# A graph layer on one core: fewer row loads on SP, more on ACT, and a block's own rows asked for a block earlier

## The chip, the cores and the metric

One core of a Trainium2 chip. The metric is the device time of one execution in microseconds (us), the median of three runs. The engines have these names: PE (TensorE, matmuls), DVE (VectorE), ACT (ScalarE), POOL (GpSimd) and SP (SyncE, which computes nothing and issues DMAs). ACT and POOL also issue DMAs, each in its own in-order queue, between their other instructions.

## The reference

12,500 nodes with 128 features each, 200,000 edges sorted by their target node. A normalized copy of the nodes is averaged over the edges that reach each node, and a small network follows, whose result is added to x:

```python
h = jnp.maximum(_layernorm(x, axis=-1), 0.0)
msgs = h[src]
agg = jax.ops.segment_sum(msgs, dst, num_segments=n)
deg = jax.ops.segment_sum(ones, dst, num_segments=n)
agg = agg / jnp.maximum(deg, 1.0)[:, None]
g = jax.nn.relu(agg @ Wg + h @ Ws + bg)          # 128 -> 128
g = jnp.tanh(g @ W1 + b1)                        # 128 -> 512
g = jnp.tanh(g @ W2 + b2)                        # 512 -> 512
out = x + g @ W3 + b3                            # 512 -> 128
```

## The kernel before

The kernel first computes h for all nodes and writes it to a table in DRAM, `htab` (L231 to L249). Then it goes over the edges in 1563 chunks of 128 (`for c in range(NCH)`, L662). A chunk needs 128 rows of `htab`, one for each edge, by the edge's source. DVE makes a one-hot matrix of the chunks' targets, eight chunks at a time (`onehot`), and PE multiplies rows by one-hot into a sum per target node (`add`, L438). Since the edges are sorted, 64 chunks reach about one block of 512 nodes; chunks whose targets straddle two blocks go into a sum of their own, `edge`.

The rows of a chunk come in one of four ways:

- for most chunks, by one indirect DMA of POOL (`gather`, L311, L313), into one of `AHEAD` = 44 row buffers; a gather waits until PE has used the buffer's last rows;
- for the ten groups of eight chunks for which `raw(c)` holds (between chunks 256 and 656), by gathers from x itself, made ahead of all else (L149 to L157);
- for the chunks in `slow_s`, by SP: 128 DMAs of one row (512 bytes) each, `srows`, four to a step;
- for the chunks in `slow_a`, by ACT in the same way, `arows`.

L86 to L100 choose the last two: from chunk 120 on, of every `EACH` + 1 chunks one goes to SP, and of every `EACH_A` + 1 chunks one to ACT. The addresses of single rows are loaded into registers, 32 at a time (`row_loads`, L340 to L356; the load of offsets, from `place`, is L347). L681 to L688 pace these loads: after so many gathered chunks that 128 rows fit evenly into the distance between two such chunks, `next(loading)` issues four more. SP's queue thus holds the single rows of `srows` and, between them in program order, the large DMAs: the blocks' h (`own`, `hb`, 256 KB), the blocks' x (`own_part`, `xb`) and the stores of the output (`store`, L639, called at L665; from chunk `QUICK` = 1312 on, a store enters the queue as soon as its sum has been written in the program). ACT's queue holds the `arows` between its activations and copies.

A block's own rows of h are needed with features on the partitions. `own(s)` loads them from `htab` (L499), `own_turned(s)` transposes them on PE (`pt`, L303 in the profile, which is the helper's line) and copies them out on ACT (`hT`, L510). L706 to L709 call these in the middle of each block's chunks: the next block is turned, and the block after it is loaded. So one block's time, 64 chunks, lies between a block's load and its transposes in the program:

```python
        if c % span == span // 2 and (c // span + 1) * BLK < N:
            own_turned(c // span + 1)
            if (c // span + 2) * BLK < N:
                own(c // span + 2)
```

The layers of earlier blocks are interleaved with the chunks: one step of `go_on` (L647) every two chunks up to `QUICK`, and by estimated times after it. Matmuls, ACT's instructions and SP's DMAs keep the order in which the program writes them; the tile framework's scheduler decides how the engines' orders interleave, and gives each DMA of SP and ACT one of eight semaphores in turn, on which it waits for the DMA that had it last.

A second path, `general`, is taken only where an edge falls outside its window; it isn't in these runs.

Of the kernel before, what the change touches and what calls it, by code (L numbers as in the profile page):

```python
# [22 lines left out]
F32 = mybir.dt.float32  # L23
# [8 lines left out]
P = 128  # L32
EPS = 1e-5
CPR = 16
BLK = 512
# [2 lines left out]
NRAW = 10  # L38
RAW0 = 256
STEP = 40  # L40
AHEAD = 44
SLOW0 = 120
EACH = 58
EACH_A = 76
TOGETHER = 4
LOADS = 32
LATE = 12
# [13 lines left out]
def windowed(ctx, tc, x, src, dst, Wg, Ws, bg, W1, b1, W2, b2, W3, b3, out, flag):  # L61
    nc = tc.nc
    N, D = x.shape
# [18 lines left out]
    def raw(c):  # L82
        return RAW0 <= c < RAW1 and (c - RAW0) % STEP < GRP


    slow_s, slow_a = [], []  # L86
    ns, na = 0, EACH // 2
    for c in range(SLOW0, NCH - 12):
        if raw(c):
            continue  # L90
        if ns <= 0:
            slow_s.append(c)
            ns = EACH
        elif na <= 0 and c < QUICK + EACH_A:
            slow_a.append(c)
            na = EACH_A
        else:
# [25 lines left out]
    rows_one = ctx.enter_context(tc.tile_pool(name="rows_one", bufs=4))  # L123
    rows_in = ctx.enter_context(tc.tile_pool(name="rows_in", bufs=AHEAD))
    ps_c = ctx.enter_context(tc.tile_pool(name="ps_c", bufs=1, space=PSUM))
# [56 lines left out]
    def centre(pool, xt, k, stats, bufs=2):  # L182
        nc.vector.tensor_reduce(stats[:, 0], xt, AX.X, ALU.add)
        nc.vector.scalar_tensor_tensor(xt, spread(stats[:, 0], k), -1.0 / D, xt, op0=ALU.mult, op1=ALU.add)
        sq = pool.tile([P, k, D], F32, name=f"sq{k}", bufs=bufs)
        if bufs > 1:
            nc.scalar.activation(sq, xt, AF.Square)
        else:
            nc.vector.tensor_tensor(sq, xt, xt, op=ALU.mult)
        nc.vector.tensor_reduce(stats[:, 1], sq, AX.X, ALU.add)  # L190

    def factors(stats):
        nc.scalar.activation(stats[:, 1], stats[:, 1], AF.Sqrt, bias=eps, scale=1.0 / D)
        nc.vector.reciprocal(stats[:, 1], stats[:, 1])
# [98 lines left out]
    ml = ctx.enter_context(tc.tile_pool(name="ml", bufs=2))  # L293
# [14 lines left out]
    def sp_dma(*a):  # L308
        tc.keep_in_program_order(nc.sync.dma_start(*a))  # L309
# [48 lines left out]
    def raw_stats(i):  # L358
        return stats_raw[:, :, i * GRP : (i + 1) * GRP]

    def raw_scaled(i):
        h = raw_rows[i]
        scale(h, h, GRP, raw_stats(i))
        for j in range(GRP):
            rows_t[RAW0 + i * STEP + j] = h[:, j]
# [12 lines left out]
    def onehot(g):  # L378
        k = min(GRP, NCH - g * GRP)
        lo, w = window(g * GRP)  # L380
        is_raw = raw(g * GRP)
        oh = ed.tile([P, GRP, W_RAW], F32, name="ohr", bufs=2) if is_raw else oh_bufs[g % OHS]
        if not is_raw and w < oh_w[g % OHS]:
            nc.vector.memset(oh[:, :, w : oh_w[g % OHS]], 0.0)
            oh_w[g % OHS] = w
        nc.vector.tensor_tensor(  # L386
            oh[:, :k, :w], lane[:, None, :w].to_broadcast([P, k, w]),
            dloc[:, g * GRP : g * GRP + k][:, :, None].to_broadcast([P, k, w]), op=ALU.is_equal,
        )
        ohs[g] = oh  # L390
        step, n = (oh.shape[2], w) if is_raw else (PITCH - per, w + per * (k - 1))
        cnt = ed.tile([P, PITCH], BF16, name="cnt", bufs=2)
        part, row, col = oh.ap
        shifted = bass.AP(tensor=oh.tensor, offset=oh.offset, ap=[part, [col[0], n], [step * col[0], k]])
        with nc.allow_low_precision(reason="whole numbers up to the windows that reach a node"):
            nc.vector.tensor_reduce(cnt[:, :n], shifted, AX.X, ALU.add)  # L396
            for b, (n0, m) in enumerate(blocks):
                a0, a1 = max(lo, n0), min(lo + n, n0 + m)
                if a0 < a1:
                    if b not in counts:  # L400
                        counts[b] = ed.tile([P, BLK], BF16, name="deg", bufs=3) if m > P else ed.tile(
                            [P, P], BF16, name="deg_s", bufs=4
                        )
                        nc.vector.memset(counts[b][:, :m], 0.0)
                    d = counts[b][:, a0 - n0 : a1 - n0]
                    nc.vector.tensor_tensor(d, d, cnt[:, a0 - lo : a1 - lo], op=ALU.add)  # L406
# [10 lines left out]
    def count(b):  # L417

        n, m = blocks[b]
        dg = flat(ps_m.tile([P, 4, P], F32, name="pm"))  # L420
        pe.matmul(dg[:, :m], ones, counts.pop(b)[:, :m], start=True, stop=True)
        rd = ml.tile([P, BLK], F32, name="rd", bufs=3)
        nc.vector.tensor_scalar(rd[:, :m], dg[:, :m], 1.0, None, op0=ALU.max)  # L423
        nc.vector.tensor_reduce(total[:, b : b + 1], dg[:1, :m], AX.X, ALU.add)  # L424
        nc.vector.reciprocal(rd[:, :m], rd[:, :m])  # L425
        rds[b] = rd
# [66 lines left out]
    def own(s):  # L493

        n0 = s * BLK
        n = min(BLK, N - n0)
        k = -(-n // P)
        hb = ml.tile([P, BLK // P, D], F32, name="hb", bufs=2)
        sp_dma(hb[:, :k], htab[n0 : n0 + k * P, :].rearrange("(t p) d -> p t d", p=P))  # L499
        owns[s] = hb  # L500

    def own_turned(s):

        k = -(-min(BLK, N - s * BLK) // P)
        hb = owns.pop(s)
        pt = ps_t.tile([P, BLK // P, P], F32, name="pt")
        for t in range(k):
            pe.transpose(pt[:, t, :], hb[:, t, :], ident)
        hT = ml.tile([P, BLK], F32, name="hT", bufs=3)
        act.copy(hT[:, : k * P], pt[:, :k, :].rearrange("p t n -> p (t n)"))  # L510
        hTs[s] = hT
# [124 lines left out]
    span = BLK // per  # L636
    now = at = 0

    def store(upto):  # L639
        while stores and stores[0][0] <= upto:  # L640
            sp_dma(*stores.pop(0)[1:])
# [5 lines left out]
    def go_on(w):  # L647
        nonlocal now
        if w:
# [3 lines left out]
            if w[1] is None:  # L653
                work.remove(w)

    own(0)
    own(1)
    own_turned(0)
    onehot(0)
    onehot(1)  # L660
    counted = 0
    for c in range(NCH):  # L662
        g = c // GRP
        at = c
        store(c if c >= QUICK else c - LATE)  # L665
        if c % GRP == 0 and g + 2 < ngrp:
            onehot(g + 2)
            if raw((g + 2) * GRP):
                raw_scaled(((g + 2) * GRP - RAW0) // STEP)
            if 2 <= g < 2 + NRAW:  # L670
                centre(ed, raw_rows[g - 2], GRP, raw_stats(g - 2), bufs=1)
            if g == 2 + NRAW:
                factors(stats_raw)

        while c % GRP == GRP // 2 and counted < len(blocks) and reach[counted][-1] // GRP <= g + (c >= QUICK):
            count(counted)
            counted += 1
        while nxt < len(order) and nxt < behind + AHEAD:
            gather(order[nxt])
            nxt += 1  # L680
        if not raw(c) and c not in slow:  # L681
            behind += 1
            batch = behind * P // (EACH * TOGETHER)
            if behind > SLOW0 - 3 * EACH and batch > (behind - 1) * P // (EACH * TOGETHER):
                next(loading, 0)
            batch = behind * P // (EACH_A * TOGETHER)
            if behind > 48 and batch > (behind - 1) * P // (EACH_A * TOGETHER):
                next(loading_a, 0)  # L688
        if c >= QUICK:

            there = 7.5 + 1.251 * (NRAW * GRP + order.index(c)) if c not in slow else 0
            while soonest() and max(now, soonest()[2]) < there:
                go_on(soonest())
            now = max(now, there) + 0.27
        add(c)

        lead = LEAD if c < QUICK else 2
        if done < len(blocks) and (c - lead if across[done] else c) >= reach[done][-1]:
            quick = reach[done][-1] + LEAD >= QUICK

            prev, older = (i if i >= 0 and reach[i][-1] + LEAD < QUICK else None for i in (done - 1, done - 2))
            older = None if quick and prev is None else older
            work.append([layers(done, prev, older), 0, 0, 0, quick and blocks[done][1] <= P])
            done += 1

        if c % span == span // 2 and (c // span + 1) * BLK < N:  # L706
            own_turned(c // span + 1)
            if (c // span + 2) * BLK < N:
                own(c // span + 2)  # L709
        if c < QUICK:  # L710
            if c % 2 == 0:
                go_on(work[0] if work else None)
        if c == QUICK:
            for b, (_, n) in enumerate(blocks):
                if n < BLK:
                    own_part(b)
# [379 lines left out]
```

## Time and profile before

| | |
|---|---|
| Runs | 2626.2 us median (2613.55 to 2628.77) |
| Profiled execution | 2637.74 us |
| Its span, first to last instruction | 2635.9 us |
| PE busy | 1242.7 us (47%) |
| PE weight loads (PEld) | 826.4 us (31%) |
| DVE busy | 1148.4 us (44%) |
| ACT busy | 217.6 us (8%) |
| POOL busy | 1446.6 us (55%) |
| srows, issued by SP | 2944 DMAs of 0.5 KB |
| arows, issued by ACT | 1920 DMAs of 0.5 KB |
| rows, gathered by POOL | 1445 indirect DMAs |

How to read what follows. A group line names the source line, the engine, the operation, and the tiles written and read with the count; after the bar stand busy time in us and the mean of one in ns, and after the next bar the engine's idle time just before these instructions with what ended most of it. A line of the waits is "who <- for whom: us in total, times, the longest". A timeline line gives start and duration in us, the engine, and equal instructions merged with their count; in brackets stands the idle time ahead and what ended it. SPq and ACTq are the queues in which SP and ACT issue DMAs; issuing isn't counted as busy. A line of one source line's answer gives the shortest, median and longest duration in ns and the first and last start in us.

### The profile page before, as it was taken

Reading aid. Unit: us, or ns where it says so; the run is one execution under the profiler, and the core shown is the slowest. Engines: PE = TensorE matmul, PEld = TensorE weight load, DVE = VectorE, ACT = ScalarE, POOL = GpSimd, SP = SyncE. Lnnn points to the kernel's source line nnn. Section 1 sums busy time; section 2 is a strip of 40 time slices with the busy share of each in tenths; the row PEclk is TensorE's granted clock in tenths of the full one; section 3 lists DMA queues with packets and bytes.
Section 4 is the critical chain, followed back from the end, with each engine's and each line's share of the span. In section 5 each row is a group of like instructions: output and inputs, shape, how many; then the busy total and the mean of one; then the engine's idle time right before and its main releaser. Section 6 shows DMA issues by size and latency. Waiting matters only on the chain. (4 is left out here: it accounts for less than half of the span.)

```text
span 2635.9 us, 24714 instructions
## 1 busy us (share of the span) xinstructions
PE 1242.7 (47%) x4838; PEld 826.4 (31%) x4838; DVE 1148.4 (44%) x1143; ACT 217.6 (8%) x352; POOL 1446.6 (55%) x1533
## 2 busy tenths in 40 slices
PE   0224334264466446545635535445244545555658
PEld 0113223142234224323323323223122323333437
DVE  5816843443454455434344343343423435334342
ACT  1100000000000001000000000000000000011012
POOL 7666665554464446546646556455554556555660
PEclk9996667686677778767767767667676777777878
DMA  6611111111121111211111111112111111121220
GB/s 173 177 44 45 50 47 41 46 41 39 43 56 44 43 47 49 53 45 50 52 47 46 50 46 49 43 38 52 45 44 45 42 49 49 44 62 46 59 61 14
DMA packets 128694, 139.69 MB, mean 53 GB/s; under 512 B 35036, under 2 KB 103294, under 8 KB 128336
## 3 DMA queue, kind: packets, MB, share of 16 engines
q0 software_dynamic: 48800, 100.04, 15.0%
q1 hardware_dynamic: 72654, 33.65, 4.6%
q10 hardware_dynamic: 7076, 4.32, 0.6%
q14 instruction: 123, 1.01, 0.1%
q8 instruction: 41, 0.67, 0.1%
HBM read 125.07 MB, written 12.82 MB: 52 GB/s over the span
## 5 line engine op out<-in xcount | busy, mean ns | idle before, releaser
L313 POOL DMA_INDIRECT rows<-htab,scol x1445 | 1368.7, 947 | 1104.0 <-PE agg L300 445.9
L300 PE MATMUL pm<-h,w 128*128 128x512 f32 (+4 forms) x1344 | 709.2, 625 | 256.2 <-issue 102.2
L386 DVE TENSOR_TENSOR oh<-shared,dloc 128x1152 f32<-128x1152 f32 (+2 forms) x186 | 244.4, 1320 | 1089.1 <-remote 409.0
L396 DVE TENSOR_REDUCE cnt<-oh 128x200 bf16<-128x1600 f32 (+2 forms) x186 | 522.9, 2817 | 3.7
L300 PEld LDWEIGHTS agg<-oh,rows 128*128 128x128 f32 x2068 | 374.7, 224 | 351.6 <-issue 328.9
L300 PE MATMUL agg<-oh,rows 128*128 128x144 f32 (+3 forms) x2068 | 400.7, 323 | 123.6 <-issue 105.8
L300 PEld LDWEIGHTS pm<-h,w 128*128 128x128 f32 x1344 | 241.5, 219 | 304.0 <-issue 139.1
L303 PE MATMUL pt<-ident,hb 128*128 128x128 f32 x98 | 25.4, 410 | 486.9 <-DMA hb<-htab 449.8
L300 PE MATMUL edge<-oh,rows 128*128 128x144 f32 (+2 forms) x822 | 176.0, 326 | 97.0 <-issue 95.1
L300 PEld LDWEIGHTS edge<-oh,rows 128*128 128x128 f32 x822 | 157.3, 226 | 203.4 <-issue 197.6
L303 PEld LDWEIGHTS pt<-ident,hb 128*128 128x128 f32 x98 | 16.9, 209 | 493.7 <-issue 486.4
L332 ACT ACTIVATE h<-pm,b2c 128x512 f32<-128x512 f32 (+4 forms) x112 | 70.6, 632 | 857.9 <-remote 202.1
L332 ACT ACTIVATE h<-pm,b1c 128x512 f32<-128x512 f32 (+4 forms) x112 | 69.5, 632 | 367.8 <-DMA arows<-htab 96.1
L153 POOL DMA_INDIRECT raw<-in_x_dram,rsrc x80 | 77.0, 962 | 25.5 <-issue 24.1
L425 DVE RECIPROCAL rd<-rd 128x512 f32<-128x512 f32 (+4 forms) x28 | 81.8, 2920 | 0.0
L300 PE MATMUL agg<-oh,srows 128*128 128x144 f32 (+1 forms) x32 | 10.9, 438 | 142.9 <-DMA srows<-htab 108.4
L487 DVE TENSOR_TENSOR mT<-agg,sums 128x136 f32<-128x136 f32 (+6 forms) x57 | 15.0, 267 | 141.6 <-remote 55.3
L335 ACT COPY hT<-pt 128x512 f32<-128x512 f32 (+1 forms) x25 | 14.4, 576 | 582.8 <-PE pt L303 393.6
L406 DVE TENSOR_TENSOR deg<-deg,cnt 128x200 bf16<-128x200 bf16 (+5 forms) x279 | 54.0, 220 | 3.4
L423 DVE TENSOR_SCALAR rd<-pm 128x512 f32<-128x512 f32 (+4 forms) x28 | 17.3, 618 | 84.2 <-remote 64.6
L300 PEld LDWEIGHTS agg<-oh,srows 128*128 128x128 f32 x32 | 7.1, 275 | 147.8 <-issue 76.7
L300 PE MATMUL pm<-mT,wg 128*128 128x512 f32 (+4 forms) x56 | 28.7, 596 | 45.0 <-issue 23.0
(79 smaller groups left out, 513.1 us busy)
## 6 DMA issues: line engine op xcount, KB each, us to landing
srows<-htab SPq DMA_DIRECT2D x2944, 0.5 KB
arows<-htab ACTq DMA_DIRECT2D x1920, 0.5 KB
rows<-htab,scol POOLq DMA_INDIRECT x1445
hb<-htab SPq DMA_DIRECT2D x24, 256.0 KB
xb<-in_x_dram SPq DMA_DIRECT2D x23, 256.0 KB
out_dram<-o SPq DMA_DIRECT2D x23, 256.0 KB
htab<-h SPq DMA_DIRECT2D x6, 896.0 KB
xt<-in_x_dram SPq DMA_DIRECT2D x5, 896.0 KB
```

The source lines that it names most:

```text
L153: nc.gpsimd.indirect_dma_start(out=t[:, j, :], out_offset=None, in_=x, in_offset=bass.IndirectOffsetOnAxis(ap=rsrc[:, g, j : j + 1], axis=0),)
L300: tc.keep_in_program_order(nc.tensor.matmul(*a, **k))
L303: tc.keep_in_program_order(nc.tensor.transpose(*a, **k))
L313: nc.gpsimd.indirect_dma_start(out=r, out_offset=None, in_=htab, in_offset=bass.IndirectOffsetOnAxis(ap=scol[:, c : c + 1], axis=0),)
L332: tc.keep_in_program_order(nc.scalar.activation(*a, **k))
L335: tc.keep_in_program_order(nc.scalar.copy(*a))
L386: nc.vector.tensor_tensor(oh[:, :k, :w], lane[:, None, :w].to_broadcast([P, k, w]), dloc[:, g * GRP : g * GRP + k][:, :, None].to_broadcas ...
L396: nc.vector.tensor_reduce(cnt[:, :n], shifted, AX.X, ALU.add)
L406: nc.vector.tensor_tensor(d, d, cnt[:, a0 - lo : a1 - lo], op=ALU.add)
L423: nc.vector.tensor_scalar(rd[:, :m], dg[:, :m], 1.0, None, op0=ALU.max)
L425: nc.vector.reciprocal(rd[:, :m], rd[:, :m])
L487: nc.vector.tensor_tensor(out, s, t, op=ALU.add)
```

## The change

SP gets 19 chunks in place of 23, ACT 18 in place of 15, POOL 1446 gathers in place of 1445. Four row buffers of POOL's are given up (2 KB a partition), and `hb` gets a third buffer (2 KB a partition). A block's h is loaded one block earlier.

```diff
-AHEAD = 44
+AHEAD = 40
 SLOW0 = 120
-EACH = 58
-EACH_A = 76
+EACH = 72
+EACH_A = 64
...
-        hb = ml.tile([P, BLK // P, D], F32, name="hb", bufs=2)
+        hb = ml.tile([P, BLK // P, D], F32, name="hb", bufs=3)
...
     own(0)
     own(1)
+    own(2)
     own_turned(0)
...
             own_turned(c // span + 1)
-            if (c // span + 2) * BLK < N:
-                own(c // span + 2)
+            if (c // span + 3) * BLK < N:
+                own(c // span + 3)
```

## The prediction, made before the changed kernel ran

> **What bounds the kernel now.** I read the page's groups first, then the waits, then a block's timeline, then SP's own waits. The groups show that no compute engine is full:
>
> ```profile
> L313 POOL DMA_INDIRECT rows<-htab,scol x1445 | 1368.7, 947 | 1104.0 <-PE agg L300 445.9
> L303 PE MATMUL pt<-ident,hb 128*128 128x128 f32 x98 | 25.4, 410 | 486.9 <-DMA hb<-htab 449.8
> ```
>
> POOL, the busiest, idles 1104 us, and 446 of them end when PE frees a row buffer. PE idles 487 us before 98 small transposes, and a load of hb ends 450 of them. The list of waits says the same of the others:
>
> ```profile
> PE pt L303 <- DMA hb<-htab: 449.8, 18, 40.1
> POOL rows L313 <- PE agg L300: 445.9, 129, 24.4
> ACT hT L335 <- PE pt L303: 393.6, 17, 39.5
> ...
> PE agg L300 <- DMA srows<-htab: 125.2, 8, 25.7
> ```
>
> Is hb slow, or asked for late? The timeline around one block's transposes answers:
>
> ```profile
> 1155.80 12.32 SPq L309 DMA_DIRECT2D srows<-htab  x28
> 1168.22 0.41 SPq L309 DMA_DIRECT2D hb<-htab  x1
> ...
> 1171.20 1.09 PE L303 MATMUL pt<-ident,hb 128*128 128x128 f32 x4 [38.61 <-DMA hb<-htab]
> ...
> 1172.33 0.58 ACT L335 COPY hT<-pt 128x512 f32<-128x512 f32 x1 [22.41 <-PE pt L303]
> ...
> 1174.75 0.94 POOL L313 DMA_INDIRECT rows<-htab,scol  x1 [20.67 <-PE agg L300]
> ```
>
> PE transposes 3 us after SP issues the load, having stood idle for 38.6 us: the load is quick, SP is late. It is behind because it issues single rows without pause; what it waits for itself is little:
>
> ```profile
> SPq L309 <- DMA arows<-htab: 89.2, 65, 5.7
> SPq L309 <- DMA srows<-htab: 44.4, 92, 1.4
> ```
>
> SP's 2944 row loads run from 114 to 2559 us, 0.83 us each. So the rate at which SP's queue issues is the bound, and PE, ACT and POOL wait in turn behind it. That rate isn't constant. In the stretch above POOL stood still and SP issued 28 rows in 12.3 us; while POOL gathered every 1.25 us from 1602.4 to 1628.6 (21 gathers) SP got through 16:
>
> ```profile
> 1602.33 25.70 SPq L309 DMA_DIRECT2D srows<-htab  x16
> ```
>
> Counted over the timeline: in 78 stretches of eight gathers 1.25 us apart SP issued 1.34 DMAs a gather; in POOL's pauses over 4 us, 733 in 362 us, or 2.02 a us. A check: of 59.8 chunks 58 are gathered, and SP has 128 rows and 2.8 large DMAs (hb, xb, out) to issue. 58 gathers take 72.5 us, in which SP issues 78; the other 53 need 26.3 us of pauses. That gives 98.8 us, or 1.70 us a gather. The blocks between 1171.2 and 2145.6 us took 108.3 us with some 62 gathers: 1.74. The law holds within 3%.
>
> **The change part by part.** *SP's rows.* srows falls from 2944 to 2432 and its loads of row offsets from 92 to 76. A period is now 72 gathers, with 131.4 DMAs on SP. ACT's rows get denser, 1.94 a gather for 1.66; in the counted stretches SP issued 1.40 a gather where ACT issued 1.2 and 1.25 where ACT issued 1.8, so I lower 1.34 to 1.27. 72 gathers take 90 us, in which SP issues 91; the other 40 need 19.8 us. 109.8 us, or 1.525 a gather: 10.3% less than 1.70. SP's law governs from its first row (114 us) to about chunk 1312 (2257 us, that block's transposes), 2143 us: **-221 us**. Bounds: without ACT's influence 1.49 a gather, 12.3%, -264. The other way: when ACT has no rows left (2227 to 2450 us) SP issues 1.53 a us against 1.27 with 0.97 of ACT's, both at the same share of POOL; that is 0.134 us an SP issue, or 0.175 an ACT row. 430 fewer SP rows up to there at 1/2.02 us give -213, and 384 more ACT rows +67: -146. I keep -221, since the stretches are the nearest rows.
>
> The loads of row offsets lie in these counts, so they are not added again. Their row:
>
> ```profile
> L347 SPq TENSOR_LOAD <-place x92: 343/2113/2469, 111.6 to 2536.4; - x92
> ```
>
> By it the 16 that go are 34 of the 221 us. The Trainium skill (Runtime: NRT & Kernel Launch, Instruction fetch mechanics) puts such a load at about 200 ns a register even in bulk; with 32 registers that would be 6.4 us each and 102 us for the 16. The measured 2.1 us decides.
>
> *ACT's rows*, 1920 to 2304. From 260 to 2227 us ACT's timeline holds 1249 us of row issuing without any wait (1880 rows, 0.66 us each), 145 us of ACTIVATEs and copies, and 573 us of waiting. 384 rows more are 254 us, and they fit into that waiting only if PE comes to it earlier. That they do I price at no cost by themselves; the cover is the 573 us. If it doesn't open, the fourth case below applies.
>
> *The two queues' shared semaphores.* In the built program each DMA of SP or ACT waits for one of eight semaphores dealt out in turn over both queues. SP's DMA follows one of ACT's on its semaphore in 861 of 3046 cases (28%), after the change in 864 of 2534 (34%); ACT's follows SP's in 857 of 1979, then 860 of 2362. An SP row that waits so holds up the srows and the hb behind it. Before, that is the 89.2 us above. Bounds: -89 (the waits go when ACT no longer stands before hT) and +89 (they double with a busier ACT). I take **+45**: ACT is fuller, and that decides.
>
> *hb two blocks ahead.* In the built order hb's load stood where its transposes stand; after, 66 to 150 chunk matmuls lie between, and the srows are complete some 70 chunks ahead of their use instead of 1 to 3. PE's 450 us at hb go. I credit them with nothing: while SP is the bound, PE reaches its srows or ACT's late outputs instead, and waits there. The third buffer is free when it is asked for: the block that held it was turned before.
>
> *AHEAD 44 to 40* lets POOL stop 4 gathers (5 us) sooner in a pause of PE. POOL's 1104 idle us cover it; without that cover it is 5 us for each of 25 blocks, 125 us. One gather more costs 1.25 us, hidden alike.
>
> *The tail.* From chunk 1312 a store enters SP's queue as soon as its sum exists (L665), so an SP that has caught up waits for DVE there; all the rows, hb and xb queued behind it wait too. Before, those waits on o come to 20 us. Bounds +20 and, if SP's law holds there too, -25; I take 0.
>
> Sum: -221 + 45 = -176. The profiled execution took 2637.74 us (span 2635.9), 11.5 over the median of the runs. 2637.7 - 176 = 2462, less 11.5: **2450 us**.
>
> A page speaks against all this: the Trainium skill (DMA: Bandwidth & Descriptors, Issuing engines are not separate DMA queues) says that all issuing engines end on the same 16 DMA engines, so that spreading DMAs saves only issue time, usually small beside the transfer. Here the DMA engines are busy 10 to 20% of most slices and issue time is what SP lacks, so I don't follow it; by it only the total would count.
>
> **The rivals.**
> 1. *The forecast*: SP stays the bound at about 1.53 us a gather. 2450, own range 2370 to 2530. For it: SP's queue never rests in the timeline. Chance 0.50.
> 2. *SP falls out of the way* once it runs ahead, and ACT bounds: 2304 x 0.664 + 190 us of its own work in the loop = 1720 us from its first row (206 us), ending at 1926 instead of 2227. -301: 2325. For it: most of PE's idle time is behind SP. Against: SP's law above. POOL's floor is lower still: 1526 gathers x 1.25 + 113 ahead of the loop + 60 behind = 2080. Chance 0.17.
> 3. *The two queues act as one*, by a shared path or by the semaphores, and only their total counts: 4864 to 4736 row loads, 2.6% of 2445 us, -64: 2562. For it: SP slows when ACT issues more. Against: it slows by a quarter of a DMA for each of ACT's, not by one. Chance 0.18.
> 4. *Slower: ACT becomes the path.* Its 254 us more stand ahead of activations in one in-order queue, and PE waits for these. It decides if ACT's 573 us of waiting shrink by less than 254. If only the 163 us ahead of hT's copy go, the kernel is 91 us slower: 2717. For it: ACT's issues are already stretched to 0.66 us. Against: PE waits for ACT's h only 32 us now. Chance 0.13; and 0.02 that the row and hb edits cancel.
>
> **How the numbers follow.** About 1% is what a measurement of this kernel can tell from no change. 1 and 2 and most of 3 are faster by more: 0.81. Within 1%, between 2600 and 2652: what is left of 3 and the cancelling, 0.06. Slower: 0.13. The range takes in 2 below and 3 above with their scatter, 2300 to 2600, and leaves out 4 and the ends of 2.
>
> **What would show it.** Right: hb gone from PE's waits; SP's row loads in 2432 issues still without rest, near 0.9 us each; PE's waits on srows or on ACT's h grown; blocks after chunk 672 in about 97 us instead of 108. Wrong: SP with long waits of its own on arows (3 or 4); ACT issuing without rest while PE waits for h (2 or 4); blocks near 88 us (2).

## The result, and the profile after

The changed kernel took 2521.28 us (median of 4 runs, 2511.11 to 2526.76) against 2623.6 us (4 runs) before: ratio 0.961, 95% interval 0.9563 to 0.9657. The forecast was 2450, range 2300 to 2600. The profiled execution took 2511.11 us (span 2509.3), 126.6 less than the one before. That is more than the 102 us between the medians: the profile before is of an execution slower than the others (2637.74 us), the profile after of the fastest of four.

The experiments below ran later and on three chips where the kernel before takes 1935 us and not 2624, so each is read against the runs of the kernel before on its own chip; that difference is itself a part of what they found.

The same groups of the profile after:

```profile
L313 POOL DMA_INDIRECT rows<-htab,scol x1446 | 1369.1, 947 | 984.9 <-PE agg L300 359.8
L300 PE MATMUL pm<-h,w 128*128 128x512 f32 (+4 forms) x1344 | 731.8, 642 | 574.6 <-ACT h L332 343.0
...
L303 PE MATMUL pt<-ident,hb 128*128 128x128 f32 x98 | 18.0, 310 | 42.9 <-DMA hb<-htab 30.5
```

The idle time ahead of the transposes is gone (487 us, now 43), and another has come up: PE's matmuls of the layers stand idle for 575 us, mostly until ACT has delivered h. The list of waits of the kernel after:

```profile
ACT h L332 <- DMA arows<-htab: 686.1, 105, 31.6
...
PE pm L300 <- ACT h L332: 520.0, 64, 21.7
...
POOL rows L313 <- PE agg L300: 359.8, 151, 25.4
...
ACT hT L335 <- DMA arows<-htab: 209.9, 11, 33.2
```

Before, PE's wait for h was 32 us. ACT is late because of the rows that stand ahead of its activations and copies in its queue: they issue late, or wait themselves. One stretch of the timeline of the kernel after (DVE, POOL and the chunk matmuls left out) shows how that goes on to PE:

```profile
1103.93 15.87 ACTq L338 DMA_DIRECT2D arows<-htab  x12
1103.94 19.98 SPq L309 DMA_DIRECT2D srows<-htab  x25
...
1120.12 0.58 ACT L335 COPY hT<-pt 128x512 f32<-128x512 f32 x1 [26.74 <-DMA arows<-htab]
1120.20 1.21 ACTq L338 DMA_DIRECT2D arows<-htab  x4
1121.51 0.69 ACT L332 ACTIVATE h<-pm,b3c 128x512 f32<-128x512 f32 x1 [0.81 <-DMA arows<-htab]
...
1122.25 2.07 PE L300 MATMUL pm<-h,w 128*128 128x512 f32 x2 [21.71 <-ACT h L332]
```

Twelve rows take ACT 15.9 us; behind them stand the copy of hT, four rows more and the activation, and PE, idle for 21.7 us, starts 0.7 us after that activation began. More than half of the 15.9 us is one wait: the ninth row stands for 8.8 us at a semaphore whose last DMA is a row of SP's, which SP issues only at 1116.47 us. SP in turn no longer issues without rest:

```profile
SPq L309 <- DVE o L605: 234.0, 19, 19.1
SPq L309 <- DMA arows<-htab: 140.3, 77, 33.4
```

It has caught up so far that it waits for sums to store (9.4 us on this line before, 234 now), and more than before for ACT's rows on the shared semaphores (89 us before). So the transposes of the block at chunk 1312 fall at 2119.8 us instead of 2257.8: 138 us are gained up to there. The rest takes 389.5 us instead of 378.1: 11 are lost again. Most of the gain comes early: the transposes at chunk 672 fall at 1073.8 us instead of 1171.2, which is 97 us, and only 41 are added from there to chunk 1312. PE's waits for h are distributed the other way: 141 us up to 1073.8 us, 350 from there to 2119.8.

### The profile page after: what moved, and what is told of

Read it like the earlier page. It is cut to its first block, busy times and chain, and to the rows that moved or that the text cites. A ratio compares the mean times of both kernels' runs of the same rounds, so it can differ in the third digit from the quotient of the medians.

```text
span 2509.3 us, 24426 instructions
## 1 busy us (share of the span) xinstructions
PE 1286.2 (51%) x4838; PEld 842.9 (34%) x4838; DVE 1152.2 (46%) x1143; ACT 217.0 (9%) x352; POOL 1447.7 (58%) x1534
## 3 DMA queue, kind: packets, MB, share of 16 engines
q0 software_dynamic: 48832, 100.11, 15.8%
## 5 line engine op out<-in xcount | busy, mean ns | idle before, releaser
L300 PE MATMUL pm<-h,w 128*128 128x512 f32 (+4 forms) x1344 | 731.8, 642 | 574.6 <-ACT h L332 343.0
L300 PEld LDWEIGHTS agg<-oh,rows 128*128 128x128 f32 x2080 | 401.0, 237 | 575.9 <-issue 550.1
L300 PE MATMUL agg<-oh,rows 128*128 128x144 f32 (+4 forms) x2080 | 434.3, 338 | 175.3 <-issue 152.7
L300 PEld LDWEIGHTS pm<-h,w 128*128 128x128 f32 x1344 | 242.4, 222 | 626.9 <-ACT h L332 354.9
L300 PEld LDWEIGHTS edge<-oh,rows 128*128 128x128 f32 x812 | 142.6, 211 | 149.7 <-issue 145.5
L300 PE MATMUL edge<-oh,rows 128*128 128x144 f32 (+2 forms) x812 | 153.8, 307 | 53.2 <-issue 52.1
L300 PE MATMUL pm<-deg,ones 128*128 128x512 bf16 (+1 forms) x24 | 13.0, 544 | 187.0 <-ACT h L332 170.2
L300 PE MATMUL pm<-mT,wg 128*128 128x512 f32 (+4 forms) x56 | 35.2, 715 | 61.7 <-issue 26.3
L215 PE MATMUL pm<-ident,idx_f 98*128 98x98 f32 x32 | 6.2, 377 | 75.7 <-issue 69.6
L300 PE MATMUL pm<-hT,ws 128*128 128x512 f32 (+4 forms) x56 | 33.5, 680 | 14.6 <-issue 7.8
L303 PE MATMUL pt<-ident,hb 128*128 128x128 f32 x98 | 18.0, 310 | 42.9 <-DMA hb<-htab 30.5
```

The lines of the kernel that those rows point to most:

```text
L300: tc.keep_in_program_order(nc.tensor.matmul(*a, **k))
L303: tc.keep_in_program_order(nc.tensor.transpose(*a, **k))
```

## The experiments

**The two edits apart, and two variants, on a chip where the kernel before takes 1935 us.** The hb edit alone is the changed kernel with

```diff
-EACH = 72
-EACH_A = 64
+EACH = 58
+EACH_A = 76
```

> The hb edit alone (three buffers, one block earlier, 40 row buffers), with 23 chunks on SP and 15 on ACT as before. Theory 1 (SP's issue rate bounded the kernel before, and the hb wait was only where it showed): no gain, 2600 to 2650 us, PE's 450 us at hb gone from the list of waits and put down to srows, arows or h instead. Theory 2 (the early load of hb is what brought the 102 us): 2500 to 2540 us.

Measured: 1934.9 us against 1934.88; ratio 1.0006 (0.9996 to 1.0016). The split alone is the kernel before with EACH = 72 and EACH_A = 64:

> The split alone (19 chunks on SP, 18 on ACT), with hb loaded one block ahead from two buffers and 44 row buffers as before. Theory 1 (the row loads taken from SP bring the gain): 2500 to 2550 us, with PE waiting for h and for hb. Theory 2 (the early hb brings it): 2600 to 2650 us. If each is needed for the other, neither this nor the hb edit alone moves by more than a third of the 102 us.

Measured: 1935.92 us; ratio 1.0008 (0.9998 to 1.0017). Later stores:

```diff
-LATE = 12
+LATE = 40
```

> The changed kernel with the stores put 40 chunks behind their sums instead of 12 (LATE). Theory A (SP, now ahead of PE, stands at stores for sums that DVE has not made, 234 us, and holds ACT up by the shared semaphores): those 234 us fall below 60, ACT's waits on SP's semaphores fall with them, and the time is 2380 to 2460 us. Theory B (ACT's queue is full by its own issuing, so SP's waits at stores lie beside it): 2500 to 2530 us, the waits of SP moved to arows.

Measured: 1938.12 us; ratio 1.0019 (1.0009 to 1.0029). No rows on ACT:

```diff
+    slow_a = []
     slow = slow_s + slow_a
```

> The changed kernel with no rows on ACT: its 18 chunks are gathered by POOL (1464 gathers), SP keeps its 19. Theory ACT (after the change ACT's queue is the path): PE's 520 us of waiting for h fall below 100, and the time falls to where SP's law puts it without ACT's rows, 1.34 to 1.56 DMAs a gather at full POOL: 2330 to 2450 us. Theory SP (SP is still the path and ACT only looks busy): 2490 to 2530 us. Theory total (only the number of row loads of both queues counts, here halved): near POOL's floor, 2100 to 2250 us.

Measured: 1958.71 us; ratio 1.0126 (1.0109 to 1.0143). None of the four met an expectation in its numbers, since the kernel before took 26% less time than where they were thought out. Why is seen in the profile of the hb edit alone: POOL idles 441 us in all, most of it the 0.3 us between one gather and the next, so POOL's gathers are the bound there; the kernel with no rows on ACT has 18 gathers more than the split alone, 22.5 us at 1.25 us each, and takes 22.8 us more. And SP's instructions are different. The durations (shortest, median, longest, in ns) of the register move ahead of each row and of the row's DMA, first in the kernel before at 2636 us:

```profile
L309 SPq MOVE srows<-htab x2944: 1/29/1479, 113.6 to 2558.6; - x197
L309 SPq DMA_DIRECT2D srows<-htab x2944: 2/228/1398, 114.4 to 2558.6; - x197
```

and with the hb edit alone on its chip:

```profile
L309 SPq MOVE srows<-htab x2944: 29/29/29, 101.0 to 1849.8; - x197
L309 SPq DMA_DIRECT2D srows<-htab x2944: 227/228/366, 101.0 to 1849.9; - x197
```

These moves wait for no semaphore, and yet with a median of 29 ns one takes up to 1479. In the kernel before's profile 920 of SP's 5888 moves and DMAs of rows lasted 600 ns or more (656 us in all), and 292 of ACT's 3840; here none. The medians are equal. The gaps between SP's instructions are stretched too: 1115 of them were over 0.3 us without a semaphore that ended them, 839 us in all, against 51 and 18 us here. So in the runs of the forecast SP and ACT issued slowly, which is what made their queues the bound.

**The changed kernel again, and one without rows.**

> The changed kernel itself beside the kernel before. The first four kernels found the kernel before at 1935 us on their chip, where no instruction of SP lasted 600 ns and POOL gathered without a pause, against 2624 us on the chip of the forecast, where 920 did. Theory issue (SP's and ACT's stretched instructions set the time there): where the kernel before takes about 1935 us, POOL's gathers bound both and this takes 1930 to 1940 us; where it takes about 2624 us, this takes 2500 to 2540. Theory split (the change is worth its 4% on any chip): a ratio near 0.96 in either place.

Measured, on a second such chip: 1936.99 us against 1934.55; ratio 1.0017 (1.0007 to 1.0027). Theory split falls; theory issue holds in the half that could be tried: where the queues issue at full speed the change is worth nothing. SP waits there 326 us for sums to store and 322 us for ACT's rows, and that costs nothing, since POOL doesn't wait for it:

```profile
L313 POOL DMA_INDIRECT rows<-htab,scol x1446 | 1371.1, 948 | 441.2 <-issue 266.1 <-PE agg L300 70.8 <-DMA rows<-htab,scol 40.0
```

This is the same program as in the profile after, so the two can be laid side by side. First the register moves there (2521 us), then here (1937 us):

```profile
L309 SPq MOVE srows<-htab x2432: 2/29/1411, 113.8 to 2454.9; - x188
L309 SPq MOVE srows<-htab x2432: 29/29/29, 100.6 to 1859.0; - x188
```

Of SP's moves and DMAs of rows 752 lasted 600 ns or more there, and 1 here. Neither memory nor the compute engines show a difference of that size: the packets of POOL's gathers kept the DMA engines busy for 15.8% of 2509.3 us there and 20.6% of 1932.8 here, 396 and 398 us; DVE was busy for 1152 and 1155 us, and PE for 1286 there and 1312 here, though its mean granted clock was 0.762 there and 0.876 here.

The kernel without rows is the changed one with both lists empty (and the load of row offsets left out):

```diff
+    slow_s, slow_a = [], []
     slow = slow_s + slow_a
```

> The changed kernel with no chunk on SP or ACT: POOL gathers all 1483 that aren't raw. Theory issue: without row loads the stretched instructions cost nothing, and POOL's 37 more gathers are 46 us over POOL's floor: 1975 to 1990 us on either kind of chip. Theory rival (chips differ in something else, PE's clock or memory): on a chip where the kernel before takes 2600 us, this takes over 2300.

Measured: 1983.13 us; ratio 1.0254 (1.0237 to 1.0271). On this chip that is 46.1 us more than the changed kernel, and 37 gathers at 1.25 us are 46: POOL's gathers are the bound there, as theory issue has it. Whether this kernel also takes about 1983 us where the kernel before takes 2624 was not tried; no run of it fell there.

**Issuing made scarce.** To ask the question of the forecast on these chips, every row is loaded in two halves, which doubles the row DMAs that SP and ACT issue for the same bytes (the second half also costs a register addition, 33 ns on SP):

```diff
-                    dma(rb[p : p + 1, :], hbytes[bass.ds(v, ROWB)].rearrange("(o b) -> o b", o=1))
+                    for h0 in (0, ROWB // 2):
+                        dma(
+                            rb[p : p + 1, h0 : h0 + ROWB // 2],
+                            hbytes[h0:][bass.ds(v, ROWB // 2)].rearrange("(o b) -> o b", o=1),
+                        )
```

> The kernel before, with each row of SP and ACT loaded in two halves of 256 bytes: twice the DMAs for the same bytes, so that issuing is scarce on any chip. SP has 5888 + 72 of them; at the 0.33 us of an unhindered one and with the 92 loads of offsets that is 2160 us at least, 2200 to 2700 with its waits. Theory issue: POOL falls out of step, PE waits for hb as in the profile of the forecast. Theory bytes (transfers, not issues, are what SP waits for): within 3% of the kernel before.

> The changed kernel with rows in two halves. SP has 4864 + 72 DMAs, at 0.33 us 1790 us at least; ACT 4608, at 0.33 us and with 200 us of activations and 160 of offset loads 1880. Theory SP: 10 to 15% less than the kernel before in halves. Theory ACT (ACT's queue eats a part of what SP gives): 2 to 8% less, with PE waiting for ACT's h and not for hb. Theory total: 2 to 3% less.

Measured: 2976.79 us (1.5393 of the kernel before, 1.5367 to 1.5418) and 2743.82 us (1.4199, 1.4175 to 1.4223). That is 0.922 of each other (0.919 to 0.926 by the ends of the two intervals): theory ACT's 2 to 8%, at its upper end. Theory bytes falls for the first, whose time was underestimated. Now PE's longest waits, the kernel before in halves first:

```profile
PE pt L303 <- DMA hb<-htab: 699.0, 20, 60.5
PE pm L300 <- ACT h L332: 293.3, 59, 15.1
PE agg L300 <- DMA srows<-htab: 243.8, 9, 50.3
```

and the changed kernel in halves:

```profile
PE pm L300 <- ACT h L332: 1105.6, 140, 27.3
...
PE pt L303 <- DMA hb<-htab: 31.3, 1, 31.3
```

The same turn from hb to h as in the two profiles of the forecast, larger; but here PE already waits 293 us for h before the change (32 in the profile of the forecast). Halves are a stand-in: they make each row dearer by a second DMA, not by stretched instructions. The waits that lead PE's list are the same ones; that the queues bind in the same way is concluded from this likeness.

**Which edit, and which queue.** Four kernels in halves, on a third chip (kernel before 1936.29 us).

> The hb edit alone, rows in halves (23 and 15 chunks; the kernel before in halves took 2977 us, the changed one 2744). Theory 1 (the rate at which the queues issue is the bound, and an early hb gives nothing by itself): 2900 to 3010 us, PE's 699 us at hb gone and found again at ACT's h, srows or arows. Theory 2 (the early hb brings the 233 us): 2740 to 2800. Kept apart: a gain of a third to a half would make hb a part of its own.

Measured: 3008.29 us (1.5537, 1.5498 to 1.5576): about 1% more than the kernel before in halves. Where PE waits now:

```profile
PE agg L300 <- DMA srows<-htab: 672.3, 16, 72.4
PE pm L300 <- ACT h L332: 460.6, 77, 20.5
PE edge L300 <- DMA srows<-htab: 274.6, 6, 59.1
```

Its 699 us at hb are 30, and the waits for srows, 377 us before, are 947. The early load saves nothing by itself: PE gets past the transposes and stands at the next thing that SP owes it.

> The split alone, rows in halves (19 and 18 chunks, hb one block ahead from two buffers, 44 row buffers). Theory 1 (fewer rows on SP bring the gain): 2740 to 2810 us, PE's waits as in the changed kernel, at ACT's h, with less than 150 us at hb. Theory 2 (the early hb brings it): 2920 to 3000.

Measured: 2746.63 us (1.4185, 1.4148 to 1.4222), the whole gain of the changed kernel in halves, with the same waits, and no entry for hb among PE's seven longest:

```profile
PE pm L300 <- ACT h L332: 1098.4, 137, 27.6
```

With rows in halves the split brings the gain; theory 1 holds in both.

> The changed kernel in halves (2744 us) with stores 40 chunks behind their sums instead of 12. Theory A (SP's waits at stores, 99 us there and 234 us in the profile of the changed kernel, hold up ACT by the shared semaphores): 2640 to 2710 us. Theory B (they lie beside ACT's own issuing): 2725 to 2760.

Measured: 2746.79 us (1.4187, 1.4151 to 1.4223). The time is theory B's. But the edit hardly did what it was for: SP's waits for sums went from 99 to 73 us only, since SP runs on until it must wait. It leaves open what those waits cost.

> The changed kernel in halves (2744 us) without rows on ACT, 1464 gathers by POOL. Theory ACT (ACT's queue is the path after the change): PE's 1106 us of waiting for h fall below 150, and SP's law alone is left, 3.0 DMAs a gather at full POOL and 2.2 a us in POOL's pauses: 2250 to 2450 us. Theory SP (SP is still the path): 2650 to 2760. Theory total (only the number of row loads counts, here 4864 of 9472): POOL's floor, 1960 to 2050.

Measured: 2176.3 us (1.1232, 1.1204 to 1.1261), 570 us less than with ACT's rows, and below the range. PE's waits for h have left its seven longest waits; what is left is SP's:

```profile
PE agg L301 <- DMA srows<-htab: 417.3, 8, 60.7
PE edge L301 <- DMA srows<-htab: 144.1, 3, 57.2
```

(L301 is L300 of the other kernels.) So ACT's rows set the time of the changed kernel in halves, and SP is the next bound: the same kernel with whole rows took 1958.71 us, 218 us less. Taking ACT's rows away also takes them off the shared semaphores, so this run doesn't tell ACT's own issuing from its waits for SP. The trace of the changed kernel in halves tells a part: from 200 to 2400 us ACT issued rows without a wait for 1641 us, activations and copies took 145, and its rows waited 269 us for semaphores held by SP's DMAs and 138 for those of its own. No kernel here gave the two queues semaphores of their own.

The prediction's law of SP can be looked at without ACT's rows here: counted as in the prediction, 3.05 DMAs a gather at full POOL and 2.31 a us in POOL's pauses. For a period of 73.7 chunks, 72.7 of them gathered, SP has 259.5 DMAs to issue; 72.7 gathers take 90.9 us and hold 222 of them, and the other 38 take 16.3 us: 107 us, or 1.45 us a chunk. The blocks from 857.7 to 2015.8 us took 1.51. The two rates were counted in this same trace, so this checks how the law adds up and not what it foretells; with 3.0 and 2.2 the expectation came out too high.

## Why the prediction was right, and where it missed

The time, 2521, lies in the range and 71 us above the forecast: 102 us were gained, and 176 had been forecast.

The bound before: right. SP's rate of issuing set the time. With rows in halves this is shown: the edit that lightens SP's queue alone takes 2747 us where the whole change takes 2744, and the edit that answers to PE's largest wait, for hb, gains nothing. For the runs of the forecast it rests on the profiles, since the two edits were not run apart there. Crediting hb's wait with nothing was the step that mattered most: taken at its face, that wait of 450 us would have given a forecast of about 2176.

SP's law, 1.34 (1.27) DMAs a gather at full POOL and 2.02 a us in pauses, -221 us up to chunk 1312: the term that was mis-sized. With the +45 for the semaphores it makes -176 up to there, and -138 was measured between the two profiles. Up to chunk 672 the law did well: 10.3% of that stretch is 109 us, 97 were gained, and SP, counted in the same way, issued 1.25 a gather and 1.99 a us. Behind chunk 672 it failed: 112 us were due, 41 came, SP issued 1.04 a gather and 1.68 a us, and its blocks took 104.5 us instead of the 97 forecast, and 108.3 before. There SP waited 141 us for sums to store: what failed was to let SP run at its own pace while ACT's queue set another.

ACT's rows, "at no cost by themselves; the cover is the 573 us": wrong, and the likeliest cause of the miss. From 250 to 2130 us of the kernel after, ACT issued rows without a wait for about 1420 us (2250 rows, 0.63 us each), activations and copies took 147, and its rows waited 288 us for semaphores, 260 of them for one that a DMA of SP's had last (158 before). Its waits ahead of activations and copies, for PE above all, went from 396 us to under 30. So the cover did open, but to the last of it: ACT had no more slack, and with its rows ahead of its activations in one queue PE waited 520 us for it. How much of that comes from ACT's own issuing, and how much from its waits for SP, is open. The fourth rival named this mechanism and gave "PE waits for ACT's h only 32 us now" as what spoke against it; a wait that is short while ACT has 573 us of slack says nothing on what it is when the slack is gone. In halves, taking ACT's rows away saves 570 us. By the forecast's own rows ACT needed 1720 us, from 206 us on, for chunks that SP's law ended at 2036 us: 94% full, with PE behind it in every step of the layers. That could have been seen.

The shared semaphores, +45: SP's waits for arows went from 89 to 140 us, +51, which looks right as a sum but is not the same thing: 33 of it are one wait behind chunk 1312, and up to there they grew by 18. What the term left out is the other direction, ACT's rows waiting for SP's DMAs, +102 us in the loop.

The tail, 0 between +20 and -25: +11.4 between the profiles. SP's waits for sums grew there as the prediction named it, from 20 to 60 us; that they are the cause isn't shown.

AHEAD and the third buffer at nothing: the two kernels in halves that differ by both and by the early load (2744 and 2747) are the same; with the old split the same three edits took about 1% more (3008 against 2977). POOL's floor in the second rival, 2080 us, was too high: the 80 gathers from x itself end at 104 us, inside the 113 us ahead of the loop, and were counted twice. The changed kernel took 1937 us elsewhere.

In the list of what would show it, hb's going and h's coming held, and "SP without rest" did not. One of the signs against it came as well: ACT issuing with hardly a rest while PE waits for h, the second and fourth rivals' sign. So the forecast had the bound before right and the bound after only in part. That the time still fell into the range owes something to luck: ACT's queue, which the fourth rival priced at 2717 us, set a pace between that and SP's.

Not seen at all: that the slowness of issuing, on which all of this rests, belongs to the place or time of the runs. The profile before had it in one line: moves of up to 1479 ns beside a median of 29. What stretches them is open. SP issued slowly where POOL gathered (1.34 a gather of 1.25 us, 2.02 a us in pauses), yet in the profiles of two other chips POOL gathers at 1.25 us all along beside unstretched moves, so the gathers alone don't do it. No experiment here fell where they are stretched.

## What to carry to other kernels

A large wait for a load is a question about the queue that issues it: look whether the load was slow or asked for late, and if the queue is full, take work from it; with rows in halves an earlier place for the load only moved the wait. Work moved to a second in-order queue that also holds activations is priced by that queue's load up to its end, not by the waits it has now, because those vanish together with what they were waiting for. And when instructions that wait for nothing vary in duration, check on another chip before tuning to them.

## What the runs showed of the hardware that was not expected

- The kernel before took 2624 us in one place and 1935, 1935 and 1936 us on three chips; the kernel after 2521 and, on one of them, 1937. In the two profiles of the kernel after POOL's gathers took 947 and 948 ns, and the median move and DMA issue of SP 29 and 228 ns in both; the share of stretched ones differs (752 of 4864 against 1), and with it the gaps between SP's instructions that no semaphore ended (912 of over 0.3 us, 693 us in all, against 39 and 14 us).
- Twice the DMAs for the same bytes, in halves of 256 bytes, took the kernel from 1935 to 2977 us: in this kernel single-row loads cost by the issue.
- Where SP alone issued halves, one took 0.42 us on average (4864 in 2022 us, loads of offsets and large DMAs among them); with ACT issuing too, on the same eight semaphores, one took 0.53 us on SP and 0.49 us on ACT (changed kernel in halves).
- A queue can stand at a semaphore that the other queue's DMA holds before that DMA is even issued: one row of ACT's waited 8.8 us in the kernel after for a row that SP issued 7.0 us into that wait.
